# Traced arrival times in a planner's table, and products of two constant tiles in the planned idle time of TensorE

## The chip, the cores and the metric

The kernel runs on one core of a Trainium2 chip. The metric is the device time of one execution in microseconds; lower is better. The core's engines work side by side, each through its own queue in order: TensorE (PE in the profile) multiplies matrices into PSUM banks, VectorE (DVE) and ScalarE (ACT) read those banks and work elementwise, GpSimd (POOL) does elementwise work in SBUF and starts indirect DMAs, and SyncE (SP) starts most of the other DMAs. They wait for one another by semaphores.

## What is computed

The reference is two layers in a row on 4 x 1024 tokens of width 256, each wrapped in layer norms and a residual, all in f32. Cut to what matters:

```
x = x + LN(attn_layer(LN(x)))
  attn_layer: h = LN(x); q = softmax(h wq) over a head's 64 columns; k = softmax(h wk) over the 1024 tokens
              x = x + (q (k^T v)) wo + bo;  x = x + gelu(LN(x) w_ff1 + b) w_ff2 + b;  return x w_d + b_d
x = x + LN(moe_layer(LN(x)))
  moe_layer: t = rmsnorm(x); the two best of 8 experts by t gate^T, weights normalized
             each expert: the shared w1, w3, w2 plus its own low-rank parts (rank 16):
             silu(t w1 + 2 (t a1) b1) * (t w3 + 2 (t a3) b3), then w2 + 2 (. a2) b2
```

## The kernel before

The 4096 tokens form eight blocks of 512 (`BLK`), two for each of the four batches. For every block there are three streams of work. `front(i)` (L461) loads z (`load_z`, L147), normalizes it, transposes it into hT (`pt_h`), forms q (`pq`) and k (`pk`), the softmax parts, the transposes of q and k (`pt_q`, `pkt`), and the product of k with z (`pz`); DVE adds it up in `kz` (copied at L596 for a batch's first block, added at L602 for the second). After a batch's second block, `pzk`, `pctx` and `pmix` turn kz into the batch's mixing matrix. `middle(i)` (L644) does the attention product (`pa`), the norm, and the feed-forward part (`pf` through gelu on ACT, L707, then `py`). `tail` (L750) normalizes, picks experts (`pl`, `pr`) and scatters each row into groups by its pair of experts. Then eight expert batches (`ORDER`, L42) are fetched by `prepare` (L908) and computed by `experts` (L1047): base products `ph<-tT,w_s`, the low-rank additions `ph<-u,b_s` and `py<-u,b_s`, the activations (L1069 to L1072, L1129 to L1133), the down products `pya` and `py`, and the up products `po`.

Two further streams prepare weights. `prepare_attn` (L370) folds biases (`pv`, `pw`). `prepare_ff` (L395) transposes wff2 (four groups `pwt`, copied to wff2T by ACT at L403), multiplies it by wd (four groups `pwd`, copied to wff2d by DVE at L412), then forms `pbd`, `pcs` and `pbf`, which DVE reads at L421, L426 and L436. It also starts the DMA that fills `rows` with a constant (L451).

The order of instructions on PE, DVE, ACT and POOL is not found by the chip or by the compiler: the program decides it while it is built. It keeps a model of time. `now()` (L196) is the planned time on PE, the sum of the costs of its products (`mm`, L270; `flip`, L285) and of planned idle time. `V`, `A` and `G` (L203 to L222) plan work on DVE, ACT and POOL. Each stream yields the time at which it may go on; the loop at L1453 takes the first stream that can go, and where none can, `wait` (L1445) moves the clock to the next time at which one may. `ARRIVE` (L368) gives the planner the times at which the first loads are there: `front` uses z0 and z1 (L476), `prepare_attn` wqv, `prepare_ff` wff2 and wff1. These numbers don't wait for anything on the chip; they only set the order. What the chip waits for is set by the data and the banks.

[...] `psum` (L253) hands out the bank that the plan has free first, and `read_out` (L259) notes when the plan has it read. Two of the eight are the buffers of one pool (`ps`) and come in turn; the others have names of their own (`py0`, `py1`, `ph00` and so on). At the first expert batch (L1460) the other six go to the experts, and two are left. A product into a bank waits on the chip until the last reader of what was in it is done.

DVE works strictly in its written order. Block 2's statistics (L300) stand ahead of L421 in it, so that DVE waits there for block 2's z to land; the load of that z is started when block 0's z is no longer needed.

Of the kernel before, what the change touches and what calls it, by code (L numbers as in the profile page):

```python
# [15 lines left out]
P = 128  # L16
# [35 lines left out]
def sandwich_kernel(  # L52
# [23 lines left out]
    nc = tc.nc  # L76
# [20 lines left out]
    ident = wp.tile([P, P], F32, tag="ident", name="ident")  # L97
    make_identity(nc, ident)
    ones = wp.tile([P, P], F32, tag="ones", name="ones")
# [36 lines left out]
    for c in range(DC):  # L136
        t = wp.tile([P, P], F32, tag=f"cbd{c}", name=f"cbd{c}")
# [52 lines left out]
    pe, idle = [0.0], [0.0]  # L190
# [3 lines left out]
    slots, last = [0.0] * len(homes), [0]  # L194

    def now():  # L196
        return pe[0] / 2400.0 + idle[0]
# [37 lines left out]
    def catch_up(key=None, soon=None, by=None):  # L235

        while later:
            if soon is not None and max(free["G"], later[0][1]) > soon:
                break
            if by is not None and max(free["G"], now(), later[0][1]) + later[0][2] > by + 0.3:  # L240
                break
            if key is not None and key not in [k for k, *_ in later]:
                break
            what, after, cost, do = later.pop(0)
            do()
            at_end[what] = G(cost, after)
# [6 lines left out]
    def psum(name):  # L253
        last[0] = slots.index(min(slots))
        slots[last[0]] = 1e9
        pool, tag = homes[last[0]]
        return pool.tile([P, BLK], F32, tag=tag, name=name)

    def read_out(end, slot=None):  # L259

        slots[last[0] if slot is None else slot] = end
        return end
# [4 lines left out]
    def small(shape, tag, name, bufs=None):  # L267
        return sm.tile(shape, F32, tag=tag, name=name, **({"bufs": bufs} if bufs else {}))
# [24 lines left out]
    def tiles(name, n=TB):  # L293
        return (small([P, n, 6], "st", f"st_{name}", 8),
                small([P, n, 2], f"mv{name[:2]}", f"mv_{name}", 6))
# [69 lines left out]
    cs_s = wp.tile([P, D], F32, tag="cs", name="cs")  # L365


    ARRIVE = {"z0": 4.5, "z1": 7.0, "wqv": 8.5, "wff2": 10.5, "wff1": 16.0}  # L368

    def prepare_attn():  # L370


        yield ARRIVE["wqv"] + 1.0
        bv = small([P, DC], "bv", "bv", 1)
# [20 lines left out]
    def prepare_ff():  # L395
        yield ARRIVE["wff2"]
        wff2T = mp1.tile([P, DC, FF], F32, tag="actB", name="wff2T")
# [30 lines left out]
        yield 0.0  # L428
        yield ARRIVE["wff1"]

# [30 lines left out]
    def front(i):  # L461
# [13 lines left out]
        z = zs[i]  # L475
        yield now() + 2.5 if i > 1 else ARRIVE[f"z{i}"]  # L476
        st, mv = tiles(f"in{i}")
# [921 lines left out]
    with tc.manual_schedule(engines={EN.PE, EN.DVE, EN.Activation, EN.Pool}):  # L1399
        fronts = [  # L1400
            Stream(lambda i=i: i < 2 or i - 2 in summed,
                   lambda i=i: front(i))
            for i in range(NBLK)
        ]
        first = Stream(always, prepare_attn)
        once = Stream(always, prepare_ff)
        blocks = [
            Stream(lambda i=i: i < 2 or stored.get(i - 2) == 2,
                   lambda i=i: middle(i))
            for i in range(NBLK)  # L1410
        ]
        ready = [
            Stream(lambda n=n, after=after: after in routed and now() >= routed[after]
                   and (n == 0 or n - 1 in moe) and (n < 2 or n - 2 in ended),
                   lambda n=n, kind=kind, at=at: prepare(
                       n, kind, blocks_rows(kind, at)))
            for n, (kind, at, after, _) in enumerate(ORDER)
        ]

        def blocks_rows(kind, at):  # L1420

            w = 2 if kind == "H" else TB
            return [
                (slice(t, t + w), rows[a : a + w * P, :].rearrange("(t p) d -> p t d", p=P))
                for t, a in zip(range(0, TB, w), (at, at + QUOTA[1]))
            ]

        def sides():

            yield from closing  # L1430
            yield from ready
            yield from tails
            yield from fronts
            yield from blocks
            yield first
            yield once

        def side():
            catch_up(soon=now() + 0.2)
            return next((s for s in sides() if s.can()), None)  # L1440

        def filler():
            return next((s for s in finals if s.can(False)), None)

        def wait(main=None):  # L1445

            at = [s.ready for s in [*sides(), *finals, *([main] if main else [])]
                  if not s.done]
            at += [min(slots) - 0.2, *routed.values()]
            at += [max(free["G"], later[0][1])] if later else []  # L1450
            idle[0] += max(min((t for t in at if t > now()), default=now()) - now(), 0.05)

        for n, (kind, _, after, _) in enumerate(ORDER):  # L1453
            while not ready[n].done:
                s = side() or filler()
                if s:
                    s.step()
                else:
                    wait()
            del homes[2:], slots[2:]  # L1460
            main = Stream(always, lambda: experts(n, kind))
            while not main.done:
                s = side()
                if s:
                    s.step()
                elif main.can(False):
                    main.step()
                elif filler():
                    filler().step()
                else:  # L1470
                    wait(main)
        while not all(f.done for f in finals):
            s = side() or filler()
            if s:
                s.step()
            else:
                wait()
        for s in closing:
            while not s.done:
                s.step()  # L1480
        catch_up()
# [69 lines left out]
```

## Time and profile before

| | |
|---|---|
| Median of 3 runs | 1156.06 us (1155.9, 1156.06, 1159.53) |
| Profiled execution | 1165.82 us, of which the span is 1164.0 us |
| Mean granted clock of TensorE in it | 0.981 |
| PE busy | 1099.7 us (94%), 4708 records |
| Weight loads (PEld) | 743.4 us (64%) |
| DVE, POOL, ACT busy | 618.8 (53%), 393.7 (34%), 341.5 us (29%) |
| HBM read, written | 21.50 MB, 17.12 MB |
| First product on PE | 9.33 us, second group 14.42 us |
| Last product on PE ends | about 1149 us |

Times in the profile count from the span's start. A line of a timeline gives the start, the length, the engine, the source line, the operation, what is written and read, and in brackets the idle time of the engine before it with what ended that. An f32 product shows as two records, a transpose as one. The ends of products are modelled, so starts are the better measure. The granted clock is the share of its full clock that TensorE was given in a stretch. The profiled execution took 9.8 us more than the median of the runs.

### The profile page before, as it was taken

Reading aid. Unit: us, or ns where it says so; the run is one execution under the profiler, and the core shown is the slowest. Engines: PE = TensorE matmul, PEld = TensorE weight load, DVE = VectorE, ACT = ScalarE, POOL = GpSimd, SP = SyncE. Lnnn points to the kernel's source line nnn. Section 1 sums busy time; section 2 is a strip of 40 time slices with the busy share of each in tenths; the row PEclk is TensorE's granted clock in tenths of the full one; section 3 lists DMA queues with packets and bytes.
Section 4 is the critical chain, followed back from the end, with each engine's and each line's share of the span. In section 5 each row is a group of like instructions: output and inputs, shape, how many; then the busy total and the mean of one; then the engine's idle time right before and its main releaser. Section 6 shows DMA issues by size and latency. Waiting matters only on the chain. (4 is left out here: it accounts for less than half of the span.)

```text
span 1164.0 us, 13016 instructions
## 1 busy us (share of the span) xinstructions
PE 1099.7 (94%) x4708; PEld 743.4 (64%) x4708; DVE 618.8 (53%) x1736; ACT 341.5 (29%) x684; POOL 393.7 (34%) x405
## 2 busy tenths in 40 slices
PE   5989998999999999999899999999999999999894
PEld 4867887766576677676576575766446766446342
DVE  4575656647637646736548647554343453443444
ACT  3335332513422542321342322221221221221321
POOL 1010022124223232423334313572452471642642
PEclk9989999999999999999999999999999999999997
DMA  9900002101100100000011000010000000100000
GB/s 320 222 18 29 9 19 74 56 1 37 37 1 19 56 19 19 28 10 19 24 41 47 17 3 19 20 38 1 12 26 1 10 29 1 37 0 1 19 1 20
DMA packets 26180, 39.50 MB, mean 34 GB/s; under 512 B 2432, under 2 KB 19712, under 8 KB 26112
## 3 DMA queue, kind: packets, MB, share of 16 engines
q1 hardware_dynamic: 21792, 28.68, 8.0%
q0 software_dynamic: 3072, 8.51, 2.0%
q10 hardware_dynamic: 1248, 1.44, 0.4%
q8 instruction: 39, 0.64, 0.2%
q14 instruction: 29, 0.24, 0.1%
HBM read 21.50 MB, written 17.12 MB: 33 GB/s over the span
## 5 line engine op out<-in xcount | busy, mean ns | idle before, releaser
L275 PE MATMUL ph<-tT,w_s 128*128 128x512 f32 (+1 forms) x640 | 234.9, 514 | 4.8 <-DVE act L1132 2.3
L275 PEld LDWEIGHTS ph<-tT,w_s 128*128 128x128 f32 x640 | 119.5, 191 | 97.2 <-issue 75.4
L275 PE MATMUL ph<-u,b_s 64*128 64x256 f32 (+2 forms) x512 | 164.4, 511 | 2.4 <-DVE act L1071 1.2
L275 PEld LDWEIGHTS ph<-u,b_s 64*128 64x128 f32 (+1 forms) x512 | 68.8, 189 | 83.9 <-issue 66.2
L275 PE MATMUL pf<-h2T,wff_s 128*128 128x256 f32 x512 | 117.1, 384 | 2.9 <-ACT h2T L687 2.5
L275 PE MATMUL py<-wff2d,g 128*128 128x256 f32 x512 | 115.7, 379 | 0.0
L275 PEld LDWEIGHTS pf<-h2T,wff_s 128*128 128x128 f32 x512 | 97.3, 192 | 19.3 <-ACT h2T L687 2.7
L1071 DVE SCALAR_TENSOR_TENSOR act<-act,ph 128x256 f32<-128x256 f32 (+1 forms) x96 | 48.6, 506 | 114.0 <-ACT act L1069 114.0
L275 PEld LDWEIGHTS py<-wff2d,g 128*128 128x128 f32 x512 | 97.3, 190 | 13.2
L1117 POOL TENSOR_TENSOR actB<-act,act 128x512 f32<-128x512 f32 x31 | 39.9, 1286 | 155.6 <-DVE act L1072 61.6
L1117 POOL TENSOR_TENSOR actA<-act,act 128x512 f32<-128x512 f32 x32 | 41.4, 1293 | 135.2 <-DVE act L1133 69.0
L707 ACT ACTIVATE g<-pf,bff 128x256 f32<-128x256 f32 x128 | 53.3, 472 | 103.2 <-PE pf L275 103.2
L1069 ACT ACTIVATE act<-ph 128x256 f32<-128x256 f32 (+1 forms) x96 | 40.3, 452 | 134.6 <-PE ph L275 105.0
L733 DVE SCALAR_TENSOR_TENSOR x<-py,std,x 128x256 f32<-128x256 f32 x32 | 15.5, 484 | 118.4 <-PE py L275 118.4
L275 PE MATMUL py<-u,b_s 64*128 64x512 f32 x128 | 67.0, 646 | 0.0
L275 PE MATMUL po<-w_s,actA 128*128 128x256 f32 x256 | 63.2, 386 | 0.6 <-POOL actA L1117 0.6
L1332 ACT COPY py<-ph 128x512 f32<-128x512 f32 x62 | 34.9, 569 | 93.5 <-PE ph L275 85.2
L275 PE MATMUL po<-w_s,actB 128*128 128x256 f32 x256 | 62.2, 382 | 0.0
L275 PEld LDWEIGHTS po<-w_s,actA 128*128 128x128 f32 x256 | 47.2, 191 | 20.3 <-issue 12.8
L890 POOL DMA_INDIRECT rows<-x,to x32 | 32.8, 1025 | 66.4 <-DVE x L856 19.4
L275 PEld LDWEIGHTS po<-w_s,actB 128*128 128x128 f32 x256 | 47.6, 190 | 11.9 <-issue 6.1
L1072 DVE TENSOR_TENSOR act<-act,ph 128x256 f32<-128x256 f32 (+1 forms) x96 | 48.9, 509 | 5.9 <-DVE act L1071 0.5
(246 smaller groups left out, 1775.1 us busy)
## 6 DMA issues: line engine op xcount, KB each, us to landing
rows<-none SPq DMA_DIRECT2D x1, 4208.0 KB
kept<-x SPq DMA_DIRECT2D x16, 263.0 KB
x<-in_x_dram SPq DMA_DIRECT2D x8, 512.0 KB, 5.7
row<-rows SPq DMA_DIRECT2D x6, 526.0 KB, 3.8
w_s<-in_w_dram SPq DMA_DIRECT2D x3, 1024.0 KB, 13.3
z<-in_x_dram SPq DMA_DIRECT2D x6, 512.0 KB, 3.4
wff_s<-in_wff_dram SPq DMA_DIRECT2D x2, 1024.0 KB, 10.7
row<-rows SPq DMA_DIRECT2D x4, 263.0 KB, 3.7
```

What stands on the lines that cost most here:

```text
L275: nc.tensor.matmul(out_, lhsT=lhsT, rhs=rhs, start=start, stop=stop, **kw)
L707: nc.scalar.activation(g[:, k * W : (k + 1) * W], pf[:, k * W : (k + 1) * W], AF.Gelu_apprx_tanh, bias=bff1_s[:, f : f + 1],)
L733: nc.vector.scalar_tensor_tensor(y[:, j, :], py[:, D : 2 * D], std[:, j : j + 1], y[:, j, :], ALU.mult, ALU.add)
L890: ins = nc.gpsimd.indirect_dma_start(out=dst[:, :], out_offset=bass.IndirectOffsetOnAxis(ap=at, axis=0), in_=src, in_offset=None, bounds_c ...
L1069: nc.scalar.activation(th, h1, AF.Tanh, scale=0.5)
L1071: nc.vector.scalar_tensor_tensor(th, th, 1.0, h1, ALU.add, ALU.mult)
L1072: nc.vector.tensor_tensor(th, th, h3, ALU.mult)
L1117: lambda x0=x0, x1=x1, op=op: nc.gpsimd.tensor_tensor(ac, x0, x1, op))
L1332: nc.scalar.copy(py[a], ph[a])
```

## The change

It has two parts. First, the five numbers of `ARRIVE` are replaced by others: z0, z1, wqv, wff2 and wff1 are taken to be there at 4.3, 9.1, 8.6, 14.6 and 18.0 us instead of 4.5, 7.0, 8.5, 10.5 and 16.0. Second, where `wait` finds that the plan leaves PE idle until some time, it first calls `keep_warm`: if the planned time is 9 us or later, and a bank has been free in the plan for at least 0.8 us, it writes as many 128x128 f32 products of the constant tiles `ident` and `ones` as fill 0.7 of that planned idle time (less 0.3 us) at a planned cost of 4·128 cycles each, if that makes two or more. They go to a bank of their own from `psum`; nobody reads them. The plan's clock is charged with their cost and with what is left of the idle time.

```diff
-    ARRIVE = {"z0": 4.5, "z1": 7.0, "wqv": 8.5, "wff2": 10.5, "wff1": 16.0}
+    ARRIVE = {"z0": 4.3, "z1": 9.1, "wqv": 8.6, "wff2": 14.6, "wff1": 18.0}
...
+        def keep_warm(until):
+
+
+            n = int(0.7 * (until - now() - 0.3) / (4 * P / 2400.0))
+            if now() < 9.0 or n < 2 or min(slots) > now() - 0.8:
+                return
+            pw = psum("warm")
+            for _ in range(n):
+                pe[0] += 4 * P
+                nc.tensor.matmul(pw[:, 0:P], lhsT=ident, rhs=ones, start=True, stop=True)
+            read_out(now())
+
         def wait(main=None):
...
-            idle[0] += max(min((t for t in at if t > now()), default=now()) - now(), 0.05)
+            until = max(min((t for t in at if t > now()), default=now()), now() + 0.05)
+            keep_warm(until)
+            idle[0] += max(until - now(), 0.0)
```

In the built program this gives 83 products `warm<-ones,ident` in 23 places of PE's order, from the start to the last expert batch. Apart from them, the orders of PE, DVE and ACT differ only in the first part, up to the statistics of block 2: `pt_h` of block 0 comes directly after `pv`; the four `pwt` groups stand together behind block 0's `pk`; one `pwd` group follows block 0's `pkt`, and the other three stand together ahead of `pbd`. On DVE, block 0 is normalized ahead of block 1's statistics, and the copy of the fourth `pwd` group (L412) stands behind the first two statistics of block 2 instead of ahead of block 1's `qsum`. On ACT, block 1's normalization and the four copies of `pwt` stand behind block 0's exponentials. The orders of POOL and SP are the same. Lines behind L1445 move down by 14.

## The prediction

> **What bounds the kernel now.** I read the times per stretch first: TensorE (PE) is busy for 44.51 us of the 44.51 between 14.42 and 58.93, 199.41 of the next 210.07, 280.56 of 291.00 and 573.36 of 589.00. So PE's own order sets the end, and what is put on PE without a wait to cover it lengthens the kernel. Then I compared stretches that follow one another at the granted clock's own boundaries:
>
> ```profile
> 59.18:62.60 3.42, 1.60 (x10) 1.17 (x11) 1.47 (x6) 0.59 (x1) 1.01 (x1) 1.00 0.43 153
> 62.60:66.01 3.41, 2.77 (x9) 2.04 (x9) 2.51 (x10) 1.09 (x2) 0.00 (x0) 0.50 0.00 0
> 66.01:69.42 3.41, 3.40 (x13) 2.55 (x12) 2.23 (x10) 1.55 (x2) 1.98 (x2) 0.50 0.00 0
> 69.42:72.84 3.42, 3.42 (x15) 2.74 (x15) 1.90 (x3) 0.63 (x1) 0.00 (x0) 1.00 0.00 0
> 83.08:86.49 3.41, 2.80 (x20) 1.92 (x18) 3.27 (x15) 2.46 (x6) 1.12 (x2) 1.00 0.00 0
> 96.73:100.14 3.41, 1.37 (x10) 0.84 (x8) 1.21 (x5) 2.28 (x8) 0.00 (x0) 1.00 0.00 0
> 100.14:103.56 3.42, 2.96 (x7) 2.42 (x8) 3.28 (x13) 3.21 (x5) 0.00 (x0) 0.50 0.00 0
> ```
>
> After the length stand the busy times of PE, weight loads, DVE, ACT and POOL; third from the end is the granted clock. A stretch of 3.41 us in which PE is busy for 1.60 or less is followed by one at half clock; after 2.80 the clock stays. At half clock, 2.77 busy keeps it halved and 3.40 frees it. Third, the timeline of PE and of DVE where the two meet before block 0's context is mixed:
>
> ```profile
> 51.76 1.40 PE L288 MATMUL pt_q<-ident,q 128*128 128x128 f32 x8
> 52.95 1.92 PE L288 MATMUL pkt<-ident,k 128*128 128x128 f32 x8
> 54.69 4.24 PE L275 MATMUL pz<-z,q 128*128 128x256 f32 x16
> 60.27 0.94 PE L288 MATMUL pzk<-ident,kz 128*128 128x128 f32 x4 [1.34 <-DVE kz L602]
> ```
>
> ```profile
> 46.62 1.27 DVE L412 COPY wff2d<-pwd 128x512 f32<-128x512 f32 x2
> ...
> 55.29 0.43 DVE L300 BATCH_NORM_STATS2 st_in<-z 128x6 f32<-128x256 f32 x1 [4.72 <-DMA z<-in_x_dram]
> ...
> 56.37 0.40 DVE L421 TENSOR_TENSOR bd_s<-bd_s,pbd 128x256 f32<-128x256 f32 x1
> ...
> 59.77 0.84 DVE L602 SCALAR_TENSOR_TENSOR kz<-kz,less,pz 128x256 f32<-128x256 f32 x2
> ```
>
> DVE stands still for 4.72 us until block 2's z has landed, then works through what queued up behind it; PE meanwhile runs on, because the bank that pz (block 1) writes was emptied before that stop. That will matter.
>
> [...] 83.08 to 86.49 holds transposes alone, 2.80 us of them, and the clock stays full. [...] z of block 2, issued at 38.18 behind the 4208 KB fill of rows, is waited for until 55.29, while the median z takes 3.4 us from issue to landing.
>
> **The change, part by part.**
>
> *Price of a filler.* Before has no such product. The nearest row is pctx (128x128 f32) at full clock: four products from 121.62 to the next instruction at 122.51, so 0.22 us each, 0.44 at half clock. The built program holds 83: 18.5 us.
>
> *Arrival times, the start.* The built order moves block 0's transposes (pt_h) ahead of the four pwt groups, and pwt behind pk. Before, PE waited from 11.16 to 14.42 for wff2. After, pt_h can follow pv at 11.16: z of block 0 is normalized by about 9 us (rr_x at 7.78, then 0.73 on DVE, 1.09 on ACT). Adding up: pt_h 1.9 and pw 1.7 at half clock to 14.8; pq 3.5 and pk 3.4 to 21.7; pwt 1.75 to 23.5; the filler of six (1.3) to 24.8. Then a new wait: ACT has two k copies, two exponentials and z of block 1 to do before pt_h of block 1, to about 25.7. From there the old order plus one pwd moved later (1.73) brings pbd to about 45.7 against 46.55: 0.85 us gained. It is not kept: what follows waits for DVE, and DVE for z of block 2[...]. Issued earlier, it still lies behind the fill.
>
> *Arrival times, the collision.* In the built order the fourth wff2d copy (L412) now stands behind the first two statistics of block 2's z on DVE. The banks come round differently too: the four fillers ahead of block 1's pz take the bank of that fourth pwd, and pz itself that of pbd (before: one that L412 had emptied by 47.89). The program lists a wait on DVE for both. So: 55.29 for z, two statistics to 56.37, the copy (0.68) to 57.05. Only then four fillers (0.9) to 57.95, and pz (3.46) to 61.4. kz takes 0.84 plus about 0.05, so pzk starts at 62.3 instead of 60.27: 2.1 us late at full clock. PE stands from about 53.5 to 57.05. [...] half clock follows for 3 to 6 us[...]; on 4.3 us of work that is 1.5 to 2.8 more. I take 2.0: 4.1 late, bounds 0.6 (DVE's extra copy alone, if the banks don't bind) and 5.3. Behind the waiting filler on PE stands everything else; who waits for that is kz on DVE, then the mixing chain, and SP's load of block 3's z, which needs pz to be done (59.01 before) but is read only at 65.08. The two fillers ahead of pzk (0.44) stay inside the wait for kz. SP's and POOL's own orders don't change, and no DMA is moved past another.
>
> *Fillers in waits that exist.* Seven in the 2.51 us ahead of pf, six in the 2.20 ahead of pr at 188.01, three in the 0.65 at 1086.59, four ahead of block 3's pt_h, whose transposes had to wait anyway (1.57 us for 8), two in the tail (pya takes 2.00 instead of 1.08): no cost, while the waits last. They lift the busy part of the windows at 96.73 and 185.48 from 1.37 to 2.9 and from 1.21 to 2.5, and so save half of a 3.41 us window each: 1.7. [...] Sum 2.8; bounds 1.5 and 5.1 (three whole windows).
>
> *Fillers where PE did not wait.* The plan sees idle time where the chip has none, as ahead of a py group: the planner waits for the last gelu, but py begins with wd products and six earlier gelus. From the timeline, twos at 139.76, 158.24, 175.78 and 188.70: 1.76. Three at 219.65: 0.66. Around 196 to 201 six against waits of 0.34 and 0.79: 0.2. Three ahead of po at 552.45, with a wait of 1.64 behind: 0.2. Fives at 882.32, 1053.05 and 1099.29 against waits of 0.61, 0.60 and 0.60: 0.5 each. Sixes at 1079.96 and 1114.80 against 0.60 and 0.61: 0.7 each. Two at 67.75, hidden at full clock: 0. Sum 5.7. Later waits for engines other than PE give some back; I take 4.9, bounds 3.5 and 6.6 (all that stands in no wait, some at half clock).
>
> **The sum.** Against the profiled execution (span 1164.0, 1165.82 with what lies around it): it has nine windows at half clock between 18 us and the tail, three of which the fillers would undo, 5.1; front 3.5 (its own half clock at 62.60 offsets part), fillers 4.9: 1165.8 + 3.3 = 1169.1. The median of the runs, 1156.06, lies 9.8 lower; I put that to fewer half-clock windows. There the saving counts by its chance: 1156.06 + 4.1 + 4.9 − 2.8 = 1162.3, so 1162.
>
> **Rivals.** *The banks don't bind, and fillers pay for themselves*: z of block 2 lands sooner because it is issued 2.8 us earlier, pz starts on time (front 0.6), half of the uncovered fillers vanishes in later waits (2.9 is left), the clock gives 3.5: 1156.06 + 0.6 + 2.9 − 3.5 = 1156. For it: the earlier issue; against it: the full queue. *Faster, by the clock*: if the unprofiled runs have as many half-clock windows as the profiled one, fillers save 5.1 there and 3.4 more at 62.60; with the start's 0.85 kept and 4.0 of filler cost the time is 1156.06 − 5.1 − 3.4 − 0.85 + 4.0 = 1151. It decides from a saving above 8 us. Against it: 1156.06 is 9.8 below the profiled run, so few windows are left to save. *The change doesn't do what it says*: the fillers stand where the plan is idle but PE is not, and every window falls as before; nothing saved, front 4.1, 5.7 paid: 1166.
>
> **How the numbers follow.** Chances: forecast 0.58, fillers that save nothing 0.17, even 0.20, faster by the clock 0.05. About 0.3% (3.5 us) is what a measurement of this kernel can tell from no change. Slower by more than that, over 1159.5, is the forecast and the last rival: 0.75; within, 0.20; faster, 0.05. The range takes the even case's upper part and the bounds: low 1156.06 + 2.1 + 3.5 − 5.1 = 1156.6, high 1156.06 + 5.3 + 6.6 − 1.5 = 1166.5.
>
> **What would show it.** Right: PE's wait ahead of a warm product ends near 57.05, released by the wff2d copy L412; pzk starts after 62; DVE still restarts near 55.3; no half clock after pf at 100 and pr at 188; py groups start 0.44 later behind their fillers with no wait between. Wrong: pz of block 1 starts by 55; z of block 2 lands well before 55; or the number of half-clock windows falls by four or more.

## The result and the profile after

The changed kernel took 1165.47 us (median of 18 runs, 1162.23 to 1169.29) against 1159.8 us (18 runs, 1155.29 to 1166.16) for the kernel before: a ratio of 1.0046, 95% interval 1.0029 to 1.0062. The forecast was 1162.0, in a range of 1156.5 to 1166.5. The base that it was added to, 1156.06, was the median of three runs, and lay 3.7 us below the median of eighteen. In a later session (the third of four; the first is the one just told) the same pair gave 1166.16 against 1164.52, a ratio of 1.0017 (1.0001 to 1.0033). So the change made the kernel slower both times, by 5.3 us going by the first and 2.0 by the second ratio. Why the two differ is taken up below, and is settled only in part.

The profiled executions show no difference at all: 1165.72 us against 1165.82, with a span of 1164.0 us in both. That is not because nothing happened. First the place of the collision, by the timeline of PE:

```profile
51.81 1.04 PE L288 MATMUL pkt<-ident,k 128*128 128x128 f32 x8
58.26 2.07 PE L1454 MATMUL warm<-ones,ident 128*128 128x128 f32 x8 [5.42 <-DVE wff2d L412]
60.13 4.88 PE L275 MATMUL pz<-z,q 128*128 128x256 f32 x16
64.84 0.61 PE L1454 MATMUL warm<-ones,ident 128*128 128x128 f32 x4
65.58 0.94 PE L288 MATMUL pzk<-ident,kz 128*128 128x128 f32 x4
```

And DVE in the same stretch:

```profile
46.75 1.23 DVE L562 TENSOR_TENSOR q<-q,qsum 128x1024 f32<-128x1024 f32 x1
56.46 0.43 DVE L300 BATCH_NORM_STATS2 st_in<-z 128x6 f32<-128x256 f32 x1 [8.48 <-DMA z<-in_x_dram]
...
57.55 0.66 DVE L412 COPY wff2d<-pwd 128x512 f32<-128x512 f32 x1
58.12 0.41 DVE L421 TENSOR_TENSOR bd_s<-bd_s,pbd 128x256 f32<-128x256 f32 x1
...
65.04 0.87 DVE L602 SCALAR_TENSOR_TENSOR kz<-kz,less,pz 128x256 f32<-128x256 f32 x2 [3.43 <-PE pz L275]
```

DVE has nothing left to do at 48 us and stops for block 2's z until 56.46. The copy that would empty the fillers' bank is written behind that stop, so PE, done at 52.84, stands for 5.42 us. Before, pz ran at 54.69 without a wait. Behind the stop the clock is halved. In both traces the granted clock changes only at boundaries that lie 3.41 us or a multiple of it apart; the stretches of 3.41 us counted from such a boundary are called windows below. The one that held 0.41 us of PE was granted 1.00, the two behind it 0.50:

```profile
52.43:55.84 3.41, 0.41 (x4) 0.18 (x2) 0.00 (x0) 1.20 (x3) 0.00 (x0) 1.00 0.35 115
55.84:59.25 3.41, 0.99 (x4) 0.99 (x5) 2.72 (x9) 0.00 (x0) 0.00 (x0) 0.50 0.00 0
59.25:62.67 3.42, 3.42 (x12) 2.90 (x11) 2.29 (x8) 0.00 (x0) 0.00 (x0) 0.50 0.00 0
100.22:103.63 3.41, 3.02 (x24) 2.54 (x22) 1.18 (x4) 2.28 (x8) 0.00 (x0) 1.00 0.00 0
103.63:107.05 3.42, 2.86 (x13) 2.42 (x14) 3.21 (x13) 3.40 (x7) 0.00 (x0) 1.00 0.00 0
```

The last two lines answer to those around 100 of before. There PE was busy for 1.37 us of a window and the next ran at half clock; now the fillers bring the busy time to 3.02, and the clock stays:

```profile
101.52 1.73 PE L1454 MATMUL warm<-ones,ident 128*128 128x128 f32 x14
104.19 2.05 PE L275 MATMUL pf<-h2T,wff_s 128*128 128x256 f32 x8 [0.94 <-ACT h2T L687]
```

The wait for h2T, 2.51 us before, is 0.94 now; the fillers stand inside it. The same is seen ahead of pr (0.86 left of 2.20).

The two profiles can be added up. At the start of pf the new kernel is 3.6 us late (104.19 against 100.60). From there to the end of the last product it takes 1044.7 us against 1048.4, 3.7 less. In that part before has six windows at half clock and after has one (at 653.17). Five windows at up to 1.71 us each are 8.5 us, less the 4.9 forecast for uncovered fillers: 3.6. So a loss of 3.6 in front, 4.9 of fillers paid (the forecast's figure, not a measured one) and 8.5 of clock won come out at zero in this one pair, and the cost of the change is there all the same. Not all five windows are the fillers' doing. In a second trace of the changed kernel (third session) three windows behind pf are at half clock (301.47, 574.53 and 656.45); only those at pf, at pr and near 1090 are gone in both. There the stretch from pf to the end of the last product takes 1047.9 us, 3.2 more than in the first.

### The profile page after: what moved, and what is told of

It is laid out like the page before. It is cut to its first block, busy times and chain, and to the rows that moved or that the text cites. A ratio compares the mean times of both kernels' runs of the same rounds, so it can differ in the third digit from the quotient of the medians.

```text
span 1164.0 us, 13351 instructions
## 1 busy us (share of the span) xinstructions
PE 1106.3 (95%) x4874; PEld 756.6 (65%) x4874; DVE 619.4 (53%) x1736; ACT 340.8 (29%) x684; POOL 393.7 (34%) x405
## 3 DMA queue, kind: packets, MB, share of 16 engines
q0 software_dynamic: 3072, 8.51, 2.0%
q10 hardware_dynamic: 1248, 1.44, 0.4%
## 6 DMA issues: line engine op xcount, KB each, us to landing
rows<-none SPq DMA_DIRECT2D x1, 4208.0 KB, 25.4
```

## The experiments

Each kernel ran in five rounds beside the kernel before. Besides the median I use the list of all runs with span and granted clock of each. A window at half clock lacks 1.71 of its 3.41 us, so (1 − clock) × span / 1.707 is the number of such windows in a run; about 3.5 of them lie in the tail, after the last product (9.8 to 13.1 us of each traced span). The second, third and fourth session were on three different chips. Over their runs of the kernel before (67, 75 and 50) the span follows this number with a correlation of 0.97, 0.98 and 0.98, and 1.42, 1.50 and 1.44 us for each window. "At equal clock" below means the mean span less 1.45 us for each window outside the tail: an estimate that separates what the order of the work costs from how often the clock was halved. It is rougher for the kernels in which PE stops for z: within the runs of the change, of the arrival times alone and of the covered fillers only, the slope is 0.9 to 1.1 (correlations 0.64 to 0.79; the fillers alone have 1.6), and with these slopes their figures would be 1.6 to 2.2 us higher.

**The arrival times alone** (second session, as the next three). The table is the new one; there are no fillers.

```diff
-    ARRIVE = {"z0": 4.5, "z1": 7.0, "wqv": 8.5, "wff2": 10.5, "wff1": 16.0}
+    ARRIVE = {"z0": 4.3, "z1": 9.1, "wqv": 8.6, "wff2": 14.6, "wff1": 18.0}
```

> The new arrival times alone, no fillers. My account: pz of block 1 now takes the bank of the fourth pwd, whose copy (L412) stands behind block 2's statistics on DVE, so pz starts 2 us or more late even without a filler; pzk starts 1.1 us late at full clock, up to 4 with the half clock that follows PE's idle time. 1.0 to 4.0 us slower than before, most likely 3. Rival (only the fillers cost, the table is neutral or gains the start's 0.85 us): 0 to 1 us faster than before.

Measured 1165.23 us, ratio 1.0004 (0.9983 to 1.0025): too small to see, and the interval, 2.0 us faster to 2.9 slower, leaves room for both expectations. The cost stays undecided; what the trace shows is that the collision is there without any filler, since pz itself is given the bank of the fourth pwd group:

```profile
58.63 5.73 PE L275 MATMUL pz<-z,q 128*128 128x256 f32 x16 [3.72 <-DVE wff2d L412]
```

**The fillers alone**, with the old table (77 of them).

```diff
-    ARRIVE = {"z0": 4.3, "z1": 9.1, "wqv": 8.6, "wff2": 14.6, "wff1": 18.0}
+    ARRIVE = {"z0": 4.5, "z1": 7.0, "wqv": 8.5, "wff2": 10.5, "wff1": 16.0}
```

> The fillers alone, with the old arrival times (77 of them, none at the start). My account: fillers that stand in no wait cost 4.9, saved half-clock windows give 2.8 back, and the fillers ahead of block 1's pz take the bank that pz had, so that pz falls on that of pbd, which DVE reads behind block 2's statistics: 1 to 3 us more. 3 to 5 us slower than before. Rival (the arrival table is the whole cost, fillers pay for themselves): within 1 us of before.

Measured 1164.81 us, ratio 1.0005 (0.999 to 1.002). The 3 to 5 us that were expected are not there, and the total fits the rival: here the fillers nearly pay for themselves. They do so by the clock alone. At equal clock (the table below) this kernel is 6.6 us slower than before, of which four halved windows fewer give 5.8 back, where 2.8 was expected. Part of the 6.6 is the stop, which comes as expected. L412 stands early here (46.15), the fillers run at once, and yet PE stops. The fillers have taken the bank that pz had before, and pz is given that of pbd, whose reader L421 is behind z:

```profile
53.48 1.92 PE L1454 MATMUL warm<-ones,ident 128*128 128x128 f32 x8
58.43 5.38 PE L275 MATMUL pz<-z,q 128*128 128x256 f32 x16 [3.04 <-DVE bd_s L421]
```

So each half of the change brings the stop about by itself, through another bank, and together they bring it about once: at equal clock the halves cost 1.7 and 6.6 us, the whole change 6.1 to 6.4.

**The change with the covered fillers only.** The plan is charged for all, so the order and the banks stay; left out are the 53 products that stand where PE did not wait, or in small waits.

```diff
             for _ in range(n):
-                pe[0] += 4 * P
...
+            pe[0] += 4 * P * n
+            for _ in range(n if len(warmed) in KEPT else 0):
...
+        KEPT = (0, 2, 4, 5, 6, 10, 22, 26)
```

> The changed kernel with only the 30 fillers kept that stand in waits which the chip has (the plan is charged for all 83, so that the order of the rest is the same). My account: the front stays late by 3.5 (pz still waits for the read of pbd), no filler costs, 2.8 is saved: 0 to 2 us slower than before, about 4 us faster than the changed kernel. Rival (fillers cost by their number wherever they stand): of 18.5 us of products 11.8 are gone; slower than before by more than 2 us.

Measured 1161.71 us, ratio 0.9985 (0.9971 to 0.9998). That is 1.8 us faster than before, where 0 to 2 slower was expected. The collision is in it (pz at 58.77 behind 4.00 us of wait), and at equal clock it is 1.9 us slower than before; some three halved windows fewer turn that round.

**The change with block 2's first statistics written later.** This takes the reason of the stop away: L412, L421 and the other readers come ahead of z's statistics on DVE. The orders of PE and ACT are those of the change, all 83 fillers among them.

```diff
-        yield now() + 2.5 if i > 1 else ARRIVE[f"z{i}"]
+        yield max(now() + 2.5, 51.0 if i == 2 else 0.0) if i > 1 else ARRIVE[f"z{i}"]
```

> The changed kernel with all 83 fillers, and with block 2's first two statistics moved behind the reads of pwd, pbd, pcs and pbf on DVE: four DVE instructions change place, PE's order is the same. My account: no bank waits for block 2's z any more, pz of block 1 starts at about 54, kz follows 1.1 us after block 2's z has landed, pzk starts 0.5 to 3 us ahead of before instead of 4 or more behind it: 4 to 6 us faster than the changed kernel, within 2 us of before. Rival (the bank wait is hidden, the fillers alone make the loss): same as the changed kernel.

Measured 1161.49 us, ratio 0.9975 (0.9959 to 0.9991), further down than expected. PE has no wait ahead of the fillers any more, though z lands as late as in the change. PE, then DVE:

```profile
54.70 1.91 PE L1454 MATMUL warm<-ones,ident 128*128 128x128 f32 x8
56.40 3.80 PE L275 MATMUL pz<-z,q 128*128 128x256 f32 x16
```

```profile
57.04 0.43 DVE L300 BATCH_NORM_STATS2 st_in<-z 128x6 f32<-128x256 f32 x1 [3.85 <-DMA z<-in_x_dram]
...
60.24 0.87 DVE L602 SCALAR_TENSOR_TENSOR kz<-kz,less,pz 128x256 f32<-128x256 f32 x2 [2.03 <-PE pz L275]
```

kz waits for pz, and pz for nothing. pzk comes 3.7 us after z instead of 9.1 in the change.

**The change again**, as the base for the next three (third session).

> The changed kernel itself once more, beside the next three on one chip. My account: 4 to 7 us slower than before. In the trace, pzk starts about 9 us after block 2's z is taken up by DVE (4.98 before). Rival (the loss of the first measurement came from the chip): within 2 us of before.

Measured 1166.16 us, ratio 1.0017 (1.0001 to 1.0033). That is less than the 4 to 7 us expected, and 2.0 us is just what the rival allowed. The change itself hardly moved (mean span 1163.9 in the first session, 1164.8 here); what differs is the kernel before. The stop was even longer in this profile (7.11 us, released by L412; z at 57.57), and pzk came 8.51 us after z, where about 9 was expected.

**Later statistics, no fillers.** The change with block 2's first statistics written later, and no group kept: `KEPT = ()`.

> New arrival times, block 2's first statistics moved back, and none of the 83 fillers in the program; the plan is charged for them, so that the order of the rest stays the same. My account: the front is 1.2 us ahead of before (pzk 3.7 us after block 2's z), no filler costs, no half-clock window is saved: 0 to 3 us faster than before, and about 2 us faster than with all 83 fillers in the same order (uncovered ones cost 4.9, all of them save 2.8). Rival (the fillers pay for themselves): slower than with all 83 by 1 us or more.

Measured 1158.61 us, ratio 0.9964 (0.9947 to 0.9981): 4.2 us faster than before, where 0 to 3 was expected. At equal clock it is 2.0 us; the rest is that 1.7 windows fewer were halved, without any filler. With all 83 fillers in the same order (second session) the mean span was 1.5 us longer, near the 2 expected.

**Later statistics, 30 covered fillers.** `KEPT = (0, 2, 4, 5, 6, 10, 22, 26)`.

> The same with the 30 covered fillers only. My account: they cost nothing and save 2.8: 2 to 4 us faster than with none, 4 to 7 us faster than before, the best of these. The longest single run falls by more than the fastest. Rival (half-clock windows hardly touch the end): same as with none.

Measured 1157.57 us, ratio 0.9952 (0.9936 to 0.9968). The covered fillers are worth 1.0 us by the medians and 1.5 by the mean spans (1156.3 against 1157.8), less than the 2 to 4 that I expected. In this kernel pz starts as soon as ACT has its q, and pzk waits for nothing but z and kz:

```profile
52.79 3.72 PE L275 MATMUL pz<-z,q 128*128 128x256 f32 x16 [0.34 <-ACT q L583]
56.35 0.61 PE L1454 MATMUL warm<-ones,ident 128*128 128x128 f32 x4
58.21 0.94 PE L288 MATMUL pzk<-ident,kz 128*128 128x128 f32 x4 [1.25 <-DVE kz L602]
```

**Later statistics, 38 uncovered fillers.** `KEPT = (7, 8, 9, 11, 15, 17, 18, 19, 20, 21, 23, 24, 25)`.

> The same with 38 fillers that stand where PE has little or no wait, and no others. Price 8.5 us, of which waits cover about 3. My account: 4 to 5.5 us slower than with none, with little saved. Rival (later waits give them back): within 1.5 us of none.

Measured 1166.3 us, ratio 1.0013 (0.9997 to 1.003): 7.7 us by the medians above the version without fillers, 6.0 by the mean spans, more than the 4 to 5.5 expected. At equal clock it is 4.5; the rest is one more halved window.

**The same, each group doubled** (fourth session, as all that follow): 76 products in the same places.

```diff
-            for _ in range(n if len(warmed) in KEPT else 0):
+            for _ in range(2 * n if len(warmed) in KEPT else 0):
```

> Later statistics, only the fillers in places where the chip has no wait, each group doubled (76 instead of 38, all other orders the same). Left out: the 45 other fillers. With 38 it took 1166.3, with none 1158.61. Theory (each costs its 0.22 us on TensorE's path, less what later waits give back): 38 more are 8.4 us, of which 6 to 8.4 show, so 1172 to 1175. Rival (the fillers' cost is clock phase, not their own length): under 3 us more, below 1169.

Measured 1170.27 us (8 runs), ratio 1.0055 (1.0025 to 1.0085), between the two expectations. The runs fall in groups by their clock: three at 0.992 took 1166.3 us on the mean, three at 0.985 took 1173.5. At equal clock the second 38 cost 7.0 us of their 8.4, as the first theory had it; 2.6 us of that don't show in the mean span, because with more fillers fewer windows were halved (4.5 against 6.3). What the first 38 fall short by can be seen ahead of a `ph` group late in the kernel. These are PE without uncovered fillers, with six, and with twelve:

```profile
1077.55 3.70 PE L275 MATMUL ph<-tT,w_s 128*128 128x512 f32 x8 [0.60 <-DVE act L1132]
```

```profile
1081.49 1.60 PE L1454 MATMUL warm<-ones,ident 128*128 128x128 f32 x12
1082.94 3.60 PE L275 MATMUL ph<-tT,w_s 128*128 128x512 f32 x8
```

```profile
1078.24 2.94 PE L1454 MATMUL warm<-ones,ident 128*128 128x128 f32 x24
1081.02 3.60 PE L275 MATMUL ph<-tT,w_s 128*128 128x512 f32 x8
```

Six fillers take 1.45 us from their start to the next product (1081.49 to 1082.94), and 0.60 of it was a wait anyway; with twelve it is 2.78, and no wait is left to hide the second half. (A product leaves two records, 166 for the change's 83, hence x12 for six.)

**The kernel before again**, for its trace on another chip.

> The kernel before, unchanged, for its trace beside the others. Ratio 1.000 by definition. My theory: its spread between runs is half-clock windows; with about six of them besides the tail the time is near 1163, z of block 2 is taken by VectorE between 55 and 57, pz of block 1 has by then run or is running, and pzk comes about 5 us after z. If the front's order decides the time instead, pzk minus z would differ from 5 by more than 1.

Measured 1165.97 us, ratio 1.0001 (0.9984 to 1.0017), since it is the same program. Its trace agrees with the first one of before: z at 55.58, pz at 54.81, pzk at 60.57, nine windows at half clock ahead of the tail.

**The kernel before with the later statistics as the only edit.**

```diff
-        yield now() + 2.5 if i > 1 else ARRIVE[f"z{i}"]
+        yield max(now() + 2.5, 44.0 if i == 2 else 0.0) if i > 1 else ARRIVE[f"z{i}"]
```

> The kernel before with one edit: the first two statistics of block 2's z stand behind the readers of pbd, pcs and pbf on VectorE; TensorE's and ScalarE's orders are the same as before. Theory (VectorE's stop for z is in the front's chain even before the change): pz already starts without a wait, but kz no longer stands behind the backlog of 4.1 us that z leaves, so kz follows pz and two statistics; pzk comes 3.6 us after z instead of 5.0, or earlier: 1 to 2 us faster than before. Theory (only the changed kernel has the collision): no difference. The new arrival times' own value is the difference to the version with the later statistics, the new arrival times and no fillers (0.9964 of before): I expect 0.5 to 2 us from them, so 0.997 to 0.999 here.

Measured 1158.17 us, ratio 0.9963 (0.9946 to 0.998). The gain is larger than expected. The stop for z is a cost before the change, too: there kz stood behind the work that had queued up on DVE. Here are DVE's restart and kz, first in the kernel before (fourth session), then in the edited one:

```profile
55.58 0.43 DVE L300 BATCH_NORM_STATS2 st_in<-z 128x6 f32<-128x256 f32 x1 [4.26 <-DMA z<-in_x_dram]
...
60.07 0.84 DVE L602 SCALAR_TENSOR_TENSOR kz<-kz,less,pz 128x256 f32<-128x256 f32 x2
```

```profile
56.03 0.43 DVE L300 BATCH_NORM_STATS2 st_in<-z 128x6 f32<-128x256 f32 x1 [3.02 <-DMA z<-in_x_dram]
...
58.27 0.87 DVE L602 SCALAR_TENSOR_TENSOR kz<-kz,less,pz 128x256 f32<-128x256 f32 x2 [1.07 <-PE pz L275]
```

kz comes 2.2 us after z instead of 4.5, though z itself was later. At equal clock this is worth 1.2 us, about what was expected. The greater part of the gain is the clock: 2.8 windows fewer are halved per run (4.4 against 7.2). In the two traces pzk's wait for kz is 0.57 us instead of 2.04, and before pf's wait one window is at half clock instead of three.

**Later statistics and 30 covered fillers again**, beside this one.

> The fastest version so far again, later statistics with the 30 fillers that stand in waits (left out: the other 53), beside the kernel before and the one-edit version: 0.994 to 0.997 of before, and 1 to 4 us below the one-edit version, by the start's 0.9 and about one half-clock window less. If the gain is all from the later statistics, the two are equal within 1 us.

Measured 1157.51 us, ratio 0.995 (0.9932 to 0.9969). It is 0.7 us below the one-line edit by the medians, inside the intervals of both, where 1 to 4 was expected: of the 6.7 us that the best version gains by the mean spans, the one line gives 5.3.

All of it in one table:

| kernel | ratio to before (95%) | mean span | half-clock windows ahead of the tail | span at equal clock |
|---|---|---|---|---|
| before, sessions two, three and four | 1 | 1162.4, 1162.5, 1162.8 | 7.0, 7.0, 7.2 | 1152.3, 1152.2, 1152.4 |
| the change, sessions one and three | 1.0046 (1.0029, 1.0062); 1.0017 (1.0001, 1.0033) | 1163.9; 1164.8 | 3.6; 4.4 | 1158.7; 1158.3 |
| arrival times alone | 1.0004 (0.9983, 1.0025) | 1163.3 | 6.4 | 1154.0 |
| fillers alone | 1.0005 (0.999, 1.002) | 1163.3 | 3.0 | 1158.9 |
| change, covered fillers only | 0.9985 (0.9971, 0.9998) | 1160.2 | 4.1 | 1154.2 |
| change, later statistics | 0.9975 (0.9959, 0.9991) | 1159.3 | 2.6 | 1155.5 |
| later, no fillers | 0.9964 (0.9947, 0.9981) | 1157.8 | 5.3 | 1150.2 |
| later, covered | 0.9952 (0.9936, 0.9968); 0.995 (0.9932, 0.9969) | 1156.3; 1156.1 | 4.1; 4.0 | 1150.3; 1150.2 |
| later, uncovered | 1.0013 (0.9997, 1.003) | 1163.8 | 6.3 | 1154.7 |
| later, uncovered doubled | 1.0055 (1.0025, 1.0085) | 1168.2 | 4.5 | 1161.7 |
| before, later statistics | 0.9963 (0.9946, 0.998) | 1157.5 | 4.4 | 1151.2 |

The clocks of the 18 runs of before in the first session are not on record, so it has no entry there.

## Why the prediction was right, point by point

**The collision.** It is as forecast: PE's wait ahead of a warm product ends right behind the wff2d copy L412, which follows two statistics of z. pzk comes 9.12 us after DVE takes z, against 4.98 before, so 4.1 late, which is the forecast to a tenth. To hit the tenth was luck: in the second trace of the change it is 8.51, so 3.5 late. What was off is the date: z landed at 56.46, 1.2 later than before, though its load was issued 2.6 us earlier (35.59 against 38.18). In the trace of the change the fill of rows, issued at 29.83, took 25.4 us to land, and this z 20.8, so z was there 1.2 us after the fill. That the fill kept z from coming sooner was the author's reading, not shown: no run moved the fill. DVE took z at 55.29 and 55.58 in the two traces of before and at 56.03 to 57.93 in all others. Why it comes later in these was not tried.

**What the collision costs in time.** At equal clock the arrival times alone cost 1.7 (3.9 with the slope of their own runs). The half clock, though, is largely one that before pays as well: at 52.36 and 62.60. In the traces of the arrival times alone and of the covered fillers only, the clock is halved from 49.11 and 49.68 on, before PE stops at all, so there the stop can only have prolonged it. In the total the arrival times alone show +0.9 in mean span. The 2.0 us for half clock were too much as a difference, and the text had the reason in hand ("its own half clock at 62.60 offsets part") but took it into the sum for the profiled execution alone. Against a front without the stop, the collision costs much more: 3.9 us with covered fillers (1160.2 less 1156.3) and 4.6 to 5.5 with all (1163.9 or 1164.8 less 1159.3). These compare runs of different sessions, whose kernels before agree within 0.4.

**The start.** The forecast was 0.85 gained and not kept. Right: once the statistics are moved, so that it can be kept, the new times are worth 1.0 at equal clock (1151.2 less 1150.2). In the medians it is not to be seen (ratios 0.9963 and 0.9964).

**Covered fillers.** Their cost of nothing holds: 1150.2 without, 1150.3 with them, at equal clock. They save 1.2 windows (5.3 to 4.1), 1.7 us, where 2.8 was forecast. How likely a wait was to bring half clock, on which that 2.8 rests, was the author's estimate; no trace or run shows it.

**Uncovered fillers.** 4.9 was taken from a sum of 5.7, of which 5.3 is for the 38 that were run alone; measured 4.5 for these at equal clock (1154.7 less 1150.2). The waits that give part of it back are there, and twice as many fillers use them up.

**The clock as a whole.** This is the term that was mis-sized. With the change the number of halved windows fell from 7.0 to 4.4 in the third session, 2.6 × 1.45 = 3.8 us, and in the two profiles from nine to three, 10.2 us by the length of the windows. The text named a fall by four or more as a sign against it, and in the profiles this sign came (nine to three, and nine to five in the second trace of each): 1169.1 was forecast for the profiled execution, and 1165.72 measured, because five windows behind pf went, not three. The three that were forecast went in both traces; which of the others are halved differs from run to run.

The reading on which this count rests left out a window of its own trace. From 48.94 to 52.36 before has PE busy all the time, and still half clock follows:

```profile
48.94:52.36 3.42, 3.42 (x33) 3.42 (x33) 1.55 (x3) 0.00 (x0) 0.00 (x0) 1.00 1.07 230
52.36:55.77 3.41, 3.41 (x16) 3.01 (x15) 0.45 (x2) 2.35 (x4) 0.00 (x0) 0.50 0.39 113
```

Most of it is `pbf`, 16 products that write a single column each (128x1). No wait stands in it.

**The sum.** At equal clock the forecast is 2.1 + 4.9 = 7.0, and 6.1 to 6.4 was measured (1158.7 or 1158.3 less 1152.2 or 1152.3; the first session has no figure of its own for before), or about 8 with the slope of the change's own runs. On top of that come 2.0 − 2.8 = −0.8 for the clock; measured −3.8 in the third session, where the change costs 2.3 us in all by the mean spans. So the forecast had the two costs right, and the first session came near its 5.9 in all partly by luck: in the third, with more halved windows to save, only 2.0 to 2.3 of it was left. In the first session before was 4.7 us faster than in the third, while the change was the same within 0.7 us. By the slope that is some three halved windows fewer to begin with, so less to save: an estimate, since the clocks of those runs are not on record. The forecast's guess that the 9.8 us between the profiled run and the three shown were half-clock windows fits the same line: runs of before at a clock of 0.980 took 1168.7 us on the mean, those at 0.989 took 1159.2 to 1160.0.

**The rivals.** "Fillers pay for themselves" needed z to land sooner; it landed later. Its saving by the clock (3.5) was near the 3.8 of the third session, where the total of 2.0 is nearer to its case than to the forecast. "The change doesn't do what it says" is out: the windows at pf and pr are gone in both traces of the change. "Faster, by the clock" had its decisive point at a saving above 8 us. The profiled pair saves 8.5 behind pf, and still isn't faster, since that rival kept the start's gain and left the collision out.

**Left open.** Why before ran 4 to 5 us faster in the first session than in the three others, why z lands 0.5 to 2.6 us later in all the edited kernels, and why windows full of 128x1 products are followed by half clock.

## What to carry to other kernels

Before work is put into the planned idle time of an engine, look in the trace for whether the chip is idle there: 30 products inside real waits were free and won a window or so, 38 in waits of the plan alone cost 4.5 us at equal clock. Anything that takes a bank shifts the round of banks for what follows, so look up who reads the bank that each neighbour now gets, and what that reader stands behind in its own queue; here one line that moved a statistic behind those readers was worth more (0.9963) than all the rest. And where runs of one kernel differ by 1% through the clock, compare them at equal clock as well, since a change of half a per cent looks like anything from nothing to its full size otherwise.

## What the runs showed of the hardware

The spread between runs of one program on one chip, 10 to 11 us of 1164, follows the granted clock nearly in full (correlation 0.97 to 0.98), with no change in the program. It is just under 1%, three times the 0.3% that had to be told apart here.

How busy a window was ahead of half clock shows in part. In the changed kernel the window at 649.76 held 1.64 us of PE and was followed by half clock; the one at 298.19 held 1.74, and the clock stayed full. The border isn't sharp in these records: in the second trace of the change a window with 1.78 us (at 571.12) was followed by half clock, a window with 2.03 us (later statistics without fillers, at 60.30) too, while one with 2.04 us (the one-line edit, at 58.27) was followed by full clock.

Busy time in the records doesn't tell all of it. In nine of the fourteen traces half clock follows a window that ends between 49 and 53 us and in which PE is busy throughout; without its 128x1 products (`pbf`) each of these holds 0.4 to 1.4 us of work. In the other five these products fall on two windows, each with 1.5 us or more of other work, and the clock stays full. Whether the products of one column are the reason was not tried in a run.
